# A column of weights turned by block transposes on VectorE, and a reordered head, in a three-layer cross network

## The chip, the cores and the metric

The kernel runs on one core of a Trainium2 chip. The time is the device time of one execution in microseconds (us); medians are given with the lowest and highest run. All times in this document are of one core, so the state of a whole die plays no part, and every profiled run was a fast one with a mean granted TensorE clock of 0.995 to 1.0. Each experiment ran beside the kernel before on the same chip. TensorE multiplies matrices, VectorE and GpSimd do elementwise work, ScalarE does copies, squares and biases, SyncE issues most transfers. SBUF is the on-chip memory, PSUM the accumulators that TensorE writes.

## The reference

```python
B, F, E = 2048, 64, 16            # this input has 1024 rows of x
h = x                             # (B, 64, 16), float32
for i in range(3):                # W[i] has 128 outputs
    z = einsum('bfe,bge->bfge', x, h).reshape(B, F * fh, E)
    y = einsum('oc,bce->boe', W[i], z) + b[i]
    x_i, h = (y[:, :64], y[:, 64:]) if i < 2 else (y, y)
    xs.append(x_i)
out = concatenate(xs, axis=1).sum(axis=2) @ fc_w.T + fc_b
```

Of the last layer only the sum with the fc weights is wanted. The kernel therefore folds these weights into W2 (called V2, 64 x 64), folds V2 into W1 (called M, kept in DRAM), and needs only products of x with shifted copies of itself, contracted with W0's half and with M.

## The kernel before

The rows are cut into 32 chunks of 32. The first 75 us, the *head*, handle four chunks (c0 to c3 below are `HEAD`, numbers 2, 3, 0, 1) while the weights are still being made. For each chunk and each of four shifts j, `product` makes a tile z of 128x2048 and `half_contract` multiplies it with W0's half on TensorE. A product's second input xb is either a shifted copy made by TensorE in PSUM (c0, c1) or loaded from DRAM into SBUF (c2, c3).

```python
keep_clock(8)                                   # zeros times zeros
...
h1_weights(0, w0o[0])                           # W0's weights of j = 0: one addition on VectorE
product(c0, 0, 2, NI)
nc.scalar.copy(w0o[1], w0s[1][:, :, 1, :])
h1_weights(1, w0o[1])
product(c0, 2)
...
for j in range(NJ - 1):
    product(c1, j)
product(c1, NJ - 1, engine=nc.gpsimd)

v2r = flat_tile("v2r")[:, 0:1024].rearrange("p (n c) -> p n c", n=2)
for n in range(2):
    pv = ps.tile([128, 512], F32, tag=("y", "set")[n], name=f"pv2_{n}")
    for k in range(4):                          # fc weights times W2: V2, as rows
        nc.tensor.matmul(pv[32 * k : 32 * k + 32], fv2, w2s[n][:, k * 512 : (k + 1) * 512], ...)
    nc.scalar.copy(v2r[:, n, :], pv)
half_contract(c1, 0)

pt = ps.tile([128, F // 4, 4], F32, tag="y", name="pt")
v2q = v2r.rearrange("p n (s o) -> p (n s) o", o=F)
for q in range(F // 4):                         # 32 matmuls with a 0/1 matrix turn rows to columns
    for to in halves:
        nc.tensor.matmul(pt[to, q, :], v2q[:, q, :], pick, start=True, stop=True)
nc.scalar.copy(v2t, pt.rearrange("p q k -> p (q k)"))
half_contract(c1, 3)

# M = V2 folded into W1: 8 matmuls, 4 copies to m_sb
for j in (1, 2):
    half_contract(c1, j)
# m_sb is written to DRAM (md) in pieces, and read back skewed (ms)
head_acc(c2)
for j in range(NJ):
    product(c2, j)
for j in range(NJ):
    half_contract(c2, j)
# ... reads of ms
for j in range(NJ):
    product(c3, j)
for j in range(NJ):
    half_contract(c3, j)
keep_h1()                                       # the squares of the diagonal
```

## Time and profile before

| | before |
|---|---|
| device time, median of 3 | 491.67 us (491.55 to 491.69) |
| span of the profiled run | 489.6 us |
| TensorE, VectorE, ScalarE, GpSimd busy | 484.7, 368.4, 90.5, 11.1 us |
| squares of the head start (the end of its contractions) | 44.59 us |
| first full contraction after the head | 59.09 us |

The span is what the profile sees from the first to the last instruction; the device time is some 1.8 us longer. The lines behind these numbers are shown in the prediction. They are read like this: the chain that ended last is followed back from the last instruction, and 99% of it lies on TensorE. So only what leaves TensorE's path, or lets it start sooner, can shorten the run, and that can be no more than the change takes out of the first 75 us.

### The profile page before, as it was taken

How to read it: one execution, taken by the hardware profiler on the slowest of the kernel's cores; microseconds unless marked ns; L12 is line 12 of the kernel's file. 1: busy time of each engine (PE TensorE's matmuls, PEld its weight loads, DVE VectorE, ACT ScalarE, POOL GpSimd, SP SyncE). 2: the span in 40 equal slices, each digit the busy share in tenths (PEclk: the TensorE clock that was granted, in tenths of full speed). 3: DMA queues.
4: the chain of work that ended last, by engine and by line, in shares of the span. 5: the costliest groups of instructions: out<-in, count | busy, mean ns of one | idle time of the engine just before them, and what ended most of it. 6: DMA issues, size and time to landing. Idle time of an engine off the chain costs nothing.

```text
span 489.6 us, 4089 instructions
## 1 busy us (share of the span) xinstructions
PE 484.7 (99%) x1696; PEld 219.4 (45%) x1696; DVE 368.4 (75%) x226; ACT 90.5 (18%) x157; POOL 11.1 (2%) x19
## 2 busy tenths in 40 slices
PE   9999999999999999999999999999999999999996
PEld 5655344343244344444444344443444434444474
DVE  5796899998899988898677686767868676780311
ACT  3224302022111122112211012212022121010001
POOL 5300000000000000000000000000000000000000
PEclk9999999999999999999999999999999999999999
DMA  8977984543846263544233344333244440000000
GB/s 338 420 244 220 382 347 171 173 171 112 321 182 242 93 252 143 199 171 173 106 116 138 156 171 171 149 138 106 122 173 171 171 167 5 0 0 0 1 0 1
DMA packets 14242, 78.59 MB, mean 161 GB/s; under 512 B 3756, under 2 KB 4428, under 8 KB 5200
## 3 DMA queue, kind: packets, MB, share of 16 engines
q1 hardware_dynamic: 13084, 77.05, 41.1%
q10 hardware_dynamic: 1140, 1.29, 0.9%
q8 instruction: 13, 0.21, 0.2%
q14 instruction: 5, 0.04, 0.0%
HBM read 76.69 MB, written 1.64 MB: 160 GB/s over the span
## 4 chain that ended last, share of the span: by engine, by line
PE 99%; DVE 0%; ACT 0%; issue 0%; POOL 0%; POOLq 0%
PE acc L250 79%; PE acc L284 6%; PE q L323 6%; PE acc L272 3%; PE acc L260 2%; PE misc L105 1%; PE xp L185 1%; PE po L623 0%; PE pm L451 0%; PE pv L427 0%; PE q L272 0%; PE pt L441 0%; PE q L334 0%; PE y L277 0%; PE acc L305 0%; DVE uu L355 0%
## 5 line engine op out<-in xcount | busy, mean ns | idle before, releaser
L250 PE MATMUL acc<-z,w_all 128*128 128x512 f32 (+1 forms) x928 | 387.6, 579 | 0.0
L216 DVE TENSOR_TENSOR z<-xa,xb 128x2048 f32<-128x2048 f32 x128 | 287.8, 2285 | 49.9 <-PE acc L250 40.4
L250 PEld LDWEIGHTS acc<-z,w_all 128*128 128x128 f32 x928 | 175.4, 190 | 210.9 <-issue 207.8
L221 ACT ACTIVATE z<-xa 32x512 f32<-32x512 f32 x34 | 21.3, 625 | 329.1 <-DVE z L216 327.3
L355 DVE SCALAR_TENSOR_TENSOR uu<-acc,vs,q 64x512 f32<-64x512 f32 (+1 forms) x29 | 21.2, 732 | 59.9 <-ACT q L354 59.7
L284 PE MATMUL acc<-z,w_all 128*64 128x256 f32 x256 | 28.7, 381 | 0.0
L323 PE MATMUL q<-z,w_all 128*64 128x512 f32 x128 | 27.9, 594 | 0.0
L354 ACT COPY q<-acc 64x512 f32<-64x512 f32 (+1 forms) x29 | 16.4, 565 | 36.5 <-PE acc L250 22.9
L284 PEld LDWEIGHTS acc<-z,w_all 128*64 128x64 f32 x256 | 17.9, 137 | 11.1 <-issue 2.5
L364 DVE TENSOR_REDUCE acc<-uu 128x64 f32<-128x1024 f32 (+3 forms) x19 | 20.3, 1072 | 0.3
L233 ACT COPY xx<-xa 64x512 f32<-64x512 f32 x32 | 19.6, 613 | 0.5
L229 ACT ACTIVATE sq<-xa 32x512 f32<-32x512 f32 x28 | 17.6, 628 | 0.6
L216 DVE TENSOR_TENSOR z<-xa,xp 128x2048 f32<-128x2048 f32 (+2 forms) x8 | 13.6, 1747 | 5.2 <-PE xp L185 5.2
L323 PEld LDWEIGHTS q<-z,w_all 128*64 128x64 f32 x128 | 9.0, 137 | 18.3 <-issue 18.0
L277 PE MATMUL y<-xx,bd 64*64 64x512 f32 x64 | 15.5, 603 | 0.0
L272 PE MATMUL acc<-xx,v1w 64*64 64x512 f32 (+1 forms) x58 | 13.5, 587 | 0.0
L360 DVE SCALAR_TENSOR_TENSOR uu<-y,cx,xx 128x512 f32<-128x512 f32 x16 | 11.4, 747 | 0.3
L216 POOL TENSOR_TENSOR z<-xa,xb_gps 128x2048 f32<-128x2048 f32 x2 | 9.1, 4555 | 4.8 <-ACT xb_gps L380 2.9
L260 PE MATMUL acc<-sq,w_sq 32*128 32x512 f32 (+1 forms) x58 | 8.0, 623 | 0.0
L272 PEld LDWEIGHTS acc<-xx,v1w 64*64 64x64 f32 x58 | 3.6, 132 | 8.9 <-issue 8.8
L105 PE MATMUL misc<-bd 128*128 128x128 f32 x28 | 5.0, 347 | 1.0 <-POOL bd L99 1.0
L105 PEld LDWEIGHTS misc<-bd 128*128 128x128 f32 x28 | 4.5, 251 | 1.8 <-POOL bd L99 1.0
(63 smaller groups left out, 65.2 us busy)
## 6 DMA issues: line engine op xcount, KB each, us to landing
xa<-in_xra SPq DMA_DIRECT2D x32, 1024.0 KB, 5.0
xb<-in_xrb SPq DMA_DIRECT2D x32, 1024.0 KB, 7.1
w<-in_w2t SPq DMA_DIRECT2D x2, 1024.0 KB, 9.9
xa<-in_xra SPq DMA_DIRECT2D x2, 768.0 KB, 6.2
w1s<-in_w1h SPq DMA_DIRECT2D x1, 1024.0 KB
w1x<-in_wx SPq DMA_DIRECT2D x1, 1024.0 KB, 9.4
w0x<-in_wx SPq DMA_DIRECT2D x1, 1024.0 KB, 7.0
w0t<-in_w0r SPq DMA_DIRECT2D x1, 768.0 KB, 6.3
```

Of the source, the lines that this page charges most:

```text
L216: engine.tensor_tensor(zs[c, j][:, at, :], xas[c][:, at, :], xbs[c][j].unsqueeze(1).to_broadcast([128, last - first, N]), ALU.mult,)
L221: nc.scalar.activation(zs[c, j][SQ, 0, :], xas[c][SQ, 0, :], AF.Square)
L229: nc.scalar.activation(sqs[c // 4][at : at + 32], xas[c][0:32, 0, :], AF.Square)
L233: nc.scalar.copy(xxs[c // 2][to], xas[c][to, 0, :])
L250: nc.tensor.matmul(acc_c, w_all[:, t, w_cols(c)], zs[c, j][:, i, cols], start=(t == 0 and c % 4 < 2), stop=(t == NT - NI and c % 4 >= 2),)
L260: nc.tensor.matmul(acc_c, w_sq[at, w_cols(c)], sqs[first // 4][at, cols], start=(r >= 2), stop=(r < 2), tile_position=(32 * r, 0),)
L272: nc.tensor.matmul(acc_c[q], v1w[rows], xxs[k][rows, cols], start=False, stop=(c >= FIRST and c % 4 < 2), skip_group_check=True,)
L284: nc.tensor.matmul(accs[c][halves[n]], w_all[:, t, 0:64], zs[c, j][:, i, n * H2 : (n + 1) * H2], start=(t == 0), stop=False,)
L323: nc.tensor.matmul(q_accs[k][halves[1 - n]], w_all[:, t, 64:128], zs[2 * k + n, j][:, i, :], start=(t == 0), stop=False,)
L354: nc.scalar.copy(q[h, cols], acc_c[64 - h.start : 128 - h.start])
L355: nc.vector.scalar_tensor_tensor(uu[:, cols], acc_c[h], bh1[h], q[h, cols], ALU.add, ALU.mult)
L364: nc.vector.tensor_reduce(acc[rows, of, k, half], uus[k][rows, of, E * half.start : E * half.stop].rearrange("p k (b e) -> p k b e", e=E), ...
```

## The change

Its intent: take the 32 pick matmuls off TensorE by transposing V2 in 32x32 blocks on VectorE; start M at once afterwards; and let VectorE, which then has less time, begin the third chunk sooner and hand one more product to GpSimd. The diff, cut to its core:

```diff
     def load_xb(c, first=NJ):
-        nc.sync.dma_start(out=xb, in_=xrb[c])
+        for at in (slice(0, first), slice(first, NJ)):
+            if at.start < NJ:
+                nc.sync.dma_start(out=xb[:, at, :], in_=xrb[c, :, at, :])
...
     nc.sync.dma_start(out=w0t[:, 0, :], in_=wh)
+    load_xa(c1, slice(0, 1))
     nc.sync.dma_start(out=w0t[:, 1:NJ, :], in_=w0r)
...
-    load_chunk(c2)
+    load_xa(c2)
+    load_xb(c2, 1)
...
-    keep_clock(8)
+    keep_clock(3)          # and the 2 matmuls of a constant (the biases' share of the output), moved here from 73 us
...
-    h1_weights(1, w0o[1])
     product(c0, 2)
+    h1_weights(1, w0o[1])
...
-    for j in range(NJ - 1):
+    for j in (0, 1):
         product(c1, j)
...
-        nc.scalar.copy(v2r[:, n, :], pv)
+        nc.vector.transpose(v2r[:, n, :], pv)
+    v2q = v2r.rearrange("p n (s r) -> p (n s) r", r=32)[:, :, 0]
+    for h in range(2):
+        at = slice(32 * h, 32 * h + 32)
+        nc.vector.tensor_copy(v2t[halves[h], at], v2q[halves[h]])
+        nc.scalar.copy(v2t[halves[1 - h], at], v2q[halves[h]])
+    product(c1, 2)
     half_contract(c1, 0)
-    pt = ...               # the pick matmuls, their copy, and half_contract(c1, 3)
     # M
-    for j in (1, 2):
+    for j in (3, 1, 2):
         half_contract(c1, j)
...
+    for j in (0, 1):       # two of the fourth chunk's xb go to PSUM
+        xb3 = ps.tile([128, N], F32, tag="y", name=f"xp_{c3}_{j}")
+        nc.scalar.copy(xb3, xbs[c3][j])
+        xbs[c3][j] = xb3
...
-    for j in range(NJ):
+    product(c3, NJ - 1, engine=nc.gpsimd)
+    for j in range(NJ - 1):
         product(c3, j)
-    for j in range(NJ):
+    for j in (0, 1, 3, 2):
         half_contract(c3, j)
```

W2's order in DRAM changes to suit, and M's four PSUM buffers are chosen anew.

More of the change, by code (lines that the diff above doesn't have):

```diff
@@ L115, in cin_kernel @@
         )
-    pick = const_tile("pick", [128, 4])
-    nc.gpsimd.memset(pick, 0.0)
-    for k in range(4):
-        nc.gpsimd.memset(pick[32 * k : 32 * k + 1, k : k + 1], 1.0)
     ones = const_tile("ones", [128, 2])
@@ L145, in load_xa, with load_xb @@
         )
-    def load_xb(c):
+    def load_xb(c, first=NJ):
         xb = xp.tile([128, NJ, N], F32, tag="xb", name=f"xb_{c}")
-        nc.sync.dma_start(out=xb, in_=xrb[c])
+        for at in (slice(0, first), slice(first, NJ)):
+            if at.start < NJ:
+                nc.sync.dma_start(out=xb[:, at, :], in_=xrb[c, :, at, :])
         xbs[c] = [xb[:, j, :] for j in range(NJ)]
@@ L162, in cin_kernel @@
     nc.sync.dma_start(out=w0t[:, 0, :], in_=wh)
+    load_xa(c1, slice(0, 1))
     nc.sync.dma_start(out=w0t[:, 1:NJ, :], in_=w0r)
+    load_xa(c1, slice(1, 4))
     w0s = [w0t[:, j, :].rearrange("p (i v g) -> p i v g", v=2, g=F) for j in range(NJ)]
     xb_gps = xp.tile([128, NJ, N], F32, tag="xb", name="xb_gps")
-    load_xa(c1, slice(0, 1))
-    load_xa(c1, slice(1, 4))
     for k in range(2):
@@ L193, in cin_kernel @@
     shift_pair(c0, (2, 3))
-    keep_clock(8)
+    keep_clock(3)
+    cst = const_tile("cst", [2, 1])
+    for j in range(2):
+        nc.tensor.matmul(
+            misc[0:2, 0:1], fcol[:, j : j + 1].to_broadcast([128, 2]), bcol[:, j : j + 1],
+            start=(j == 0), stop=(j == 1),
+        )
     acc = const_tile("acc", [128, 2, NCH // 2, CB])
@@ L390, in cin_kernel @@
     product(c0, 0, 2, NI)
+    nc.scalar.activation(cst, misc[0:2, 0:1], AF.Identity, bias=fcb, scale=float(E))
     nc.scalar.copy(w0o[1], w0s[1][:, :, 1, :])
+    product(c0, 2)
     h1_weights(1, w0o[1])
-    product(c0, 2)
     for j in (2, 3):
@@ L431, in cin_kernel @@
             )
-        nc.scalar.copy(v2r[:, n, :], pv)
-    half_contract(c1, 0)
-    pt = ps.tile([128, F // 4, 4], F32, tag="y", name="pt")
-    v2q = v2r.rearrange("p n (s o) -> p (n s) o", o=F)
-    for q in range(F // 4):
-        for to in halves:
-            nc.tensor.matmul(pt[to, q, :], v2q[:, q, :], pick, start=True, stop=True)
-    nc.scalar.copy(v2t, pt.rearrange("p q k -> p (q k)"))
-    half_contract(c1, 3)
+        nc.vector.transpose(v2r[:, n, :], pv)
[5 more added lines that the diff above has]
+    product(c1, 2)
+    half_contract(c1, 0)
     m_sb = z_tile("m_sb")
-    pms = [ps.tile([128, N], F32, tag=("set", "y")[m // 2], name=f"pm_{m}") for m in range(NI)]
+    pms = [
+        ps.tile([128, N], F32, tag=tag, name=f"pm_{m}", bufs=4 if tag == "acc" else 2)
+        for m, tag in enumerate(("acc", "set", "y", "y"))
+    ]
     for m in (0, 1):
@@ L601, in cin_kernel @@
     cx = const_tile("cx", [128, 1])
-    cst = const_tile("cst", [2, 1])
     def biases():
-        pb = ps.tile([128, 2], F32, tag="set", name="pb")
-        pcx, pc = pb[:, 0:1], pb[0:2, 1:2]
+        pcx = ps.tile([128, 1], F32, tag="set", name="pcx")
         for to in halves:
             nc.tensor.matmul(pcx[to], v2t[0:64], bh2, start=True, stop=True)
-        for j in range(2):
-            nc.tensor.matmul(
-                pc, fcol[:, j : j + 1].to_broadcast([128, 2]), bcol[:, j : j + 1],
-                start=(j == 0), stop=(j == 1),
-            )
         nc.scalar.copy(cx, pcx)
-        nc.scalar.activation(cst, pc, AF.Identity, bias=fcb, scale=float(E))
     NP = NCH // 2
@@ L755 @@
         "w1h": w1q,
-        "w2t": w2.reshape(128, 2, 8, 4, F).transpose(1, 0, 3, 2, 4).reshape(2, 128, 32 * F),
+        "w2t": w2.reshape(128, 2, 2, 16, 2, 32).transpose(2, 0, 1, 4, 3, 5).reshape(2, 128, 32 * F),
         "wx1": summed(w1[:64]),
```

## The prediction

No run had shown a transpose yet: the times given for the copies into v2t and in rival B rest on the author's estimate of its length. Lengths that the trace of before does show are 0.684 us for VectorE's 128x512 product with one input in PSUM, and for a 128x2048 product 2.285 us on VectorE and 4.555 on GpSimd. That the two engines can hold each other up (rival A) was an assumption then, which the trace of before does not show.

> **What bounds the kernel now.** I read the busy table first, then the chain that ended last, then the timeline of the first 75 us, because every line of the change lies there.
>
> ```profile
> PE 484.7 (99%) x1696; PEld 219.4 (45%) x1696; DVE 368.4 (75%) x226; ACT 90.5 (18%) x157; POOL 11.1 (2%) x19
> PE 99%; DVE 0%; ACT 0%; issue 0%; POOL 0%; POOLq 0%
> ```
>
> TensorE is busy from 1.0 us to the end, and the chain never leaves it for more than the last 2 us. But busy is not the same as useful: a wait of a few tenths hides between pipelined matmuls. So I take the chain in order of time (start, length, what), where each piece is a stage of the head:
>
> ```profile
> 3.93 2.11 PE xp L185 x16
> 6.04 1.98 PE misc L105 x16
> 8.02 1.88 PE acc L284 x16
> 9.90 2.75 PE xp L185 x16
> 12.64 5.33 PE acc L284 x48
> 17.97 1.85 PE pv L427 x16
> 19.83 1.88 PE acc L284 x16
> 21.70 1.81 PE pt L441 x63
> 23.52 1.78 PE acc L284 x16
> 25.30 1.88 PE pm L451 x16
> 27.18 17.42 PE acc L284 x160
> 44.59 0.62 PE acc L305 x16
> 73.23 0.17 PE pb L610 x4
> ```
>
> A half contraction (one j of a head chunk) costs 1.73 to 1.88 us, ten of them 17.42. Three pieces are not contraction: the 8 clock-keepers at 6.04 (zeros times zeros), the 32 pick matmuls at 21.70, the constant at 73.23. And the second shift, at 9.90, takes 2.75 where the first takes 2.11 [...]: it holds a wait. The timeline (start, length, engine, what, idle before and its releaser) names it, and shows VectorE at the places that matter:
>
> ```profile
> 7.24 1.21 DVE L216 TENSOR_TENSOR z<-xa,xp 128x1024 f32<-128x1024 f32 x1
> 9.23 2.28 DVE L216 TENSOR_TENSOR z<-xa,xp 128x2048 f32<-128x2048 f32 x1
> 11.56 0.20 PEld L185 LDWEIGHTS xp<-xa,shift 64*64 64x64 f32 x4 [0.69 <-DVE z L216]
> 24.71 6.70 DVE L216 TENSOR_TENSOR z<-xa,xb 128x2048 f32<-128x2048 f32 x3 [3.50 <-DMA xb<-in_xrb]
> ```
>
> The last shift waits for a PSUM buffer until product 2 of the first chunk ends (9.23 + 2.28 = 11.51). VectorE then stands idle 3.5 us until the third chunk's xb lands at 24.7. From there it works nearly without a break to 42.3 (8 products at a pitch of 2.20 us), so the products of chunks three and four leave little room if TensorE comes sooner.
>
> [...] 12 records of clock-keepers take 2.93 us at the start, 16 take 1.98 at 6 us. [...] both GpSimd products (5.99 to 10.54, 12.47 to 17.03) lie beside products whose xb is in PSUM.
>
> **The change part by part.**
>
> *Clock-keepers, 8 to 3, plus the constant's 2 matmuls.* A matmul leaves two records, a keeper's 0.111 us apart in the trace, so three end at about 6.65, the constant at about 6.85. The first contraction then waits for its weights (VectorE 6.91 + 0.42 = 7.33) and starts at 7.40 instead of 7.95. Its tiles i = 0, 1 take 0.86; i = 2 needs the product that ends at 7.24 + 1.21 = 8.45, so it resumes at 8.52 and the shift starts near 9.48 instead of 9.83. Gain here 0.35, but the next wait swallows it.
>
> *Product 2 before the second weight sum.* VectorE goes straight from 8.42 into product 2, done at 10.70 instead of 11.51; the sum follows to 11.1. The shift's first pair ends at 10.4; its last matmul waits for the later of the two buffers, 11.15 instead of 11.57. Net gain at the start of the next contraction: 0.42, in place of the 0.35, not on top. W0's rest lands some 0.6 us later (256 KB at 420 GB/s), about 9.0, still before its sum at 10.7. VectorE is 0.4 us ahead from here.
>
> *V2.* 32 pick matmuls go: their piece runs from 21.54 to 23.37 = 1.84 us of TensorE. In their place: two transposes instead of two ScalarE copies of 0.59, then four small copies of about 0.2 in two pairs. pv is ready at about 18.6 and 19.45 (17.9 - 0.42, plus the 1.13 and 1.99 after which ScalarE could read it before). VectorE has finished two products of the second chunk by 18.6. [...] copies to 20.6. The contraction that runs meanwhile ends near 21.2, so v2t is 0.6 us early and the whole 1.84 is won.
>
> *M before j = 3.* The order only; M starts at 21.2 instead of 25.2, m_sb is complete at 24.3 instead of 28.4. TensorE's sum is unchanged. The two weight writes on SyncE's queue still stand behind the fourth chunk's xb, so M's weights gain perhaps 1.5 us, not 4. They need no more: the first sum of them was done at 42.75, needed at 45.14 before and at about 42.85 now.
>
> *VectorE's order afterwards.* Product 2 of chunk two: 20.6 to 22.85. xb's first quarter lands about 22.7 (xa's end near 22.1 plus 0.6), so the third chunk starts at 22.9 instead of 24.7: products at 25.1, 27.3, 29.5, 31.8. TensorE reaches them at 28.2, 30.0, 31.7, 33.4. In the fourth chunk j = 0, 1 take their xb from PSUM, done at 34.0 and 36.2, wanted at 35.2 and 36.9; GpSimd's j = 3 runs beside them from 31.8 to 36.4, wanted at 38.6; j = 2 to 38.6, wanted at 40.4. Every product is in time, the least slack 0.7 us. Without the GpSimd product the fourth on VectorE would end at 40.8 plus its square, too late for 40.4.
>
> *The constant at 73 us:* 0.17 less, pure gain.
>
> Sum: 0.42 + 1.84 + 0.17 = 2.4 us, all on TensorE's path; nothing after 75 us is touched. 491.67 - 2.4 = 489.2.
>
> **The rivals.** *A, GpSimd and VectorE lock each other.* If the fourth chunk's xb lands before product 3 of the third chunk starts (29.5), [...] that product then waits for 4.55 us and TensorE stalls 3 to 4 us: 492 to 493. For it: nothing in the program holds GpSimd back, only the transfer. Against: xb landed about 29.7 before, with M's writes now sharing the DMA engines it lands later, and VectorE's products follow one another with no gap. I give it one in six. *B, M waits.* If the transposes took twice my estimate, v2t would come at 21.9 and 0.7 us be lost; likewise if pm's buffer is one that product 2 of chunk two holds until 22.85 (0.8 lost). 490.0. *C, fed too late.* If M's writes push the fourth xb beyond 32, its PSUM copies (0.6 each) and products are late by as much, less the slack: 489.5 to 490.5. *D, the head holds more than I see:* if the shift's last wait vanishes entirely, 0.3 more: 488.9. A change of 2% (9.8 us) would need a stall or a gain as long as a fifth of the head; none is in sight.
>
> **Range and chances.** 489.2 if all goes as worked out; B and C make 490, A up to 493. The lower end has only timings of tenths: 488.5. I set the range at 488.5 to 491.2, somewhat skewed upwards. Chances: faster by over 2% 0.01, within 2% 0.98, slower 0.01.
>
> **What would show it.** The pick group is gone and pm starts near 21.2; the piece that was 2.75 is about 2.65 and ends near 12.2; the ten contractions from j = 3 on take 5.2 and 12.2 without a wait; the squares' matmuls (0.62) start near 42.2 instead of 44.59; [...] GpSimd's third product lasts 4.55 us and starts when the third chunk's last product ends. I am wrong if a weight load of the contractions waits for a product over half a microsecond, if GpSimd's product lasts much over 4.6, or if a VectorE product lasts much over 2.3.

## The result, and the profile after

| | before | after |
|---|---|---|
| device time, median | 491.62 us (491.55 to 491.94), 6 runs | 489.1 us (489.07 to 489.2), 6 runs |
| span | 489.6 us | 487.3 us |
| TensorE busy | 484.7 us | 482.3 us |
| squares of the head start | 44.59 us | 42.39 us |
| first full contraction | 59.09 us | 56.90 us |

The ratio is 0.9948, with a 95% interval of 0.9935 to 0.9961: the same within 2%, half a per cent faster. Here and below a ratio is the mean time of one kernel's fast runs over that of the other's in the same rounds, so it is not quite the ratio of the medians quoted.

The changed kernel's busy table and the shares of its chain, by engine:

```profile
PE 482.3 (99%) x1622; PEld 216.4 (44%) x1622; DVE 367.6 (75%) x229; ACT 90.7 (19%) x158; POOL 16.6 (3%) x15
PE 99%; DVE 0%; ACT 0%; issue 0%; POOL 0%; POOLq 0%
```

TensorE is still the bound, with 2.4 us less of work: the number that the prediction's sum gives. Its chain in order of time (start, length, what; the line numbers shift by a few, so L284 of before is L291 here, L427 is L436, L451 is L462):

```profile
3.93 3.33 PE xp L184 x16
7.26 0.86 PE misc L105 x6
...
8.30 1.88 PE acc L291 x16
10.17 2.14 PE xp L184 x16
12.31 5.33 PE acc L291 x48
17.64 1.85 PE pv L436 x16
19.50 1.88 PE acc L291 x16
21.37 1.88 PE pm L462 x16
23.25 19.14 PE acc L291 x176
42.39 0.62 PE acc L312 x16
...
70.83 0.21 PE pcx L622 x4
```

The pick group is gone and M (pm) follows the first contraction of the second chunk directly, at 21.37. Then comes one unbroken piece of 11 half contractions, 19.14 us or 1.74 each; ten took 17.42 before. So no contraction waits for a product. The three steps can be read off against the chain in the prediction: the contraction of j = 1 starts at 12.31 instead of 12.64, which is 0.33; the squares start 2.20 earlier, so V2's part is 1.87; the constant that stood behind the last but one line is gone, 0.17. Together 2.4.

The timeline of the changed kernel (start, length, engine, what, idle time before it and its releaser) shows who feeds that piece:

```profile
18.70 1.58 DVE L441 STREAM_TRANSPOSE v2r<-pv 128x512 f32<-128x512 f32 x2
20.75 2.29 DVE L223 TENSOR_TENSOR z<-xa,xp 128x2048 f32<-128x2048 f32 x1
22.95 8.89 DVE L223 TENSOR_TENSOR z<-xa,xb 128x2048 f32<-128x2048 f32 x4
30.39 5.89 POOL L223 TENSOR_TENSOR z<-xa,xb 128x2048 f32<-128x2048 f32 x1 [13.06 <-DMA xb<-in_xrb]
31.76 4.48 DVE L223 TENSOR_TENSOR z<-xa,xp 128x2048 f32<-128x2048 f32 x2
36.16 2.28 DVE L223 TENSOR_TENSOR z<-xa,xb 128x2048 f32<-128x2048 f32 x1
```

The third chunk's products start at 22.95, not 24.71, and follow one another to 31.85. Then come two products with xb in PSUM, and one more. One line is odd. GpSimd's product lasts 5.89 us, while its other two last 4.56. It starts at 30.39, in the middle of VectorE's last product of the third chunk (29.56 to 31.85), and ends at 36.28. That is 4.43 after VectorE's product ended. So the record holds 1.3 to 1.5 us (5.89 less 4.56, or 31.85 less 30.39) in which GpSimd did not get on with its product, as in the prediction's rival A, and it was VectorE's product that went first. From here on "the lock" is the name for what the records of these runs show: of two products, one on each engine and both with two SBUF inputs, one did its work only when the other had ended, and its record is longer by the wait (here 5.89 us instead of 4.56). The products with xb in PSUM do not take part: the first of them runs beside GpSimd's in 2.28. Most of the experiments go after what happens when the order is the other one.

### The profile page after: what moved, and what is told of

The parts are those of the page before. It is cut to its first block, busy times and chain, and to the rows that moved or that the text cites. A ratio compares the mean times of both kernels' runs of the same rounds, so it can differ in the third digit from the quotient of the medians.

```text
span 487.3 us, 3939 instructions
## 1 busy us (share of the span) xinstructions
PE 482.3 (99%) x1622; PEld 216.4 (44%) x1622; DVE 367.6 (75%) x229; ACT 90.7 (19%) x158; POOL 16.6 (3%) x15
## 4 chain that ended last, share of the span: by engine, by line
PE 99%; DVE 0%; ACT 0%; issue 0%; POOL 0%; POOLq 0%
PE acc L257 79%; PE acc L291 6%; PE q L330 6%; PE acc L279 3%; PE acc L267 2%; PE xp L184 1%; PE misc L105 1%; PE po L631 0%; PE pm L462 0%; PE pv L436 0%; PE q L279 0%; PE q L341 0%; PE y L284 0%; PE acc L312 0%; DVE uu L362 0%
## 5 line engine op out<-in xcount | busy, mean ns | idle before, releaser
L223 DVE TENSOR_TENSOR z<-xa,xb 128x2048 f32<-128x2048 f32 x125 | 281.0, 2285 | 45.9 <-PE acc L257 38.6
L362 DVE SCALAR_TENSOR_TENSOR uu<-acc,vs,q 64x512 f32<-64x512 f32 (+1 forms) x29 | 21.2, 731 | 59.9 <-ACT q L361 59.7
L291 PE MATMUL acc<-z,w_all 128*64 128x256 f32 x256 | 28.5, 381 | 0.0
L361 ACT COPY q<-acc 64x512 f32<-64x512 f32 (+1 forms) x29 | 16.4, 565 | 36.5 <-PE acc L257 22.9
L291 PEld LDWEIGHTS acc<-z,w_all 128*64 128x64 f32 x256 | 18.0, 137 | 11.2 <-issue 2.5
L223 DVE TENSOR_TENSOR z<-xa,xp 128x2048 f32<-128x2048 f32 (+2 forms) x10 | 18.1, 1856 | 5.9 <-PE xp L184 5.9
L284 PE MATMUL y<-xx,bd 64*64 64x512 f32 x64 | 15.5, 603 | 0.0
L223 POOL TENSOR_TENSOR z<-xa,xb 128x2048 f32<-128x2048 f32 x1 | 5.9, 5890 | 13.1 <-DMA xb<-in_xrb 13.1
L184 PE MATMUL xp<-xa,shift 64*64 64x512 f32 x32 | 5.6, 803 | 0.0
```

Of the source, the lines that this page charges most:

```text
L223: engine.tensor_tensor(zs[c, j][:, at, :], xas[c][:, at, :], xbs[c][j].unsqueeze(1).to_broadcast([128, last - first, N]), ALU.mult,)
L291: nc.tensor.matmul(accs[c][halves[n]], w_all[:, t, 0:64], zs[c, j][:, i, n * H2 : (n + 1) * H2], start=(t == 0), stop=False,)
L361: nc.scalar.copy(q[h, cols], acc_c[64 - h.start : 128 - h.start])
L362: nc.vector.scalar_tensor_tensor(uu[:, cols], acc_c[h], bh1[h], q[h, cols], ALU.add, ALU.mult)
```

## The experiments

Theory: the gain is 1.84 us from V2, 0.4 from the head's order and 0.17 from the constant, and the early xb, the new order and GpSimd's third product are there so that V2's part is not lost again. Rivals: V2 gains all by itself; or the gain comes from elsewhere; and, for the danger, GpSimd's product could block VectorE if it comes first. All twelve kernels gave correct results. They ran in three groups of four, each on a chip of its own beside the kernel before: v2_alone, v2_undone, xb_whole and xb_in_sbuf (before: 491.62 us); after_again, v2_undone_j3, whole_held and sum_first (before: 491.67); and the rest (before: 491.71).

### v2_alone: V2's part put into the kernel before

```diff
 # against before
-        nc.scalar.copy(v2r[:, n, :], pv)
+        nc.vector.transpose(v2r[:, n, :], pv)
-    pt = ...                                  # the pick matmuls and their copy
+    # the four small copies into v2t, as in the change; W2's order in DRAM too
```

> The kernel before with the V2 part alone: block transposes and four copies in place of the 32 pick matmuls, everything else as before. Theory: TensorE's own work falls by 1.84 us, but the rest of the change is what keeps it fed. In the kernel before the last product of the fourth chunk ends at 42.42 us and TensorE reaches it at 42.7; nothing here moves that product, so TensorE arrives at 40.9 and waits some 1.5 us in the fourth chunk: 491.2 to 491.5, hardly faster than before. Rival: the removed matmuls are the gain and the rest is ornament: 489.8.

Measured: 491.37 us (490.99 to 493.09, 14 runs), ratio 0.9997 (0.9989 to 1.0005). The interval holds 1, so no gain is shown, though the pick matmuls are gone. (The profiled run, 490.99, is the fastest of the 14.) The timeline of this kernel, TensorE alone, with the idle time in brackets:

```profile
39.88 1.95 PE L279 MATMUL acc<-z,w_all 128*64 128x256 f32 x16 [0.25 <-DVE z L211]
42.08 1.95 PE L279 MATMUL acc<-z,w_all 128*64 128x256 f32 x16 [0.25 <-DVE z L211]
```

Its chain, at the squares:

```profile
44.03 0.62 PE acc L300 x16
```

At the end of the fourth chunk TensorE now waits for products: its last two contractions start 2.20 us after the one before (37.68, 39.88, 42.08), which is VectorE's pitch, not their own 1.74. M starts at 23.68 instead of 25.30: the 1.84 of V2, less 0.25 by which this run's head was late (the contraction of j = 1 starts at 12.89, not 12.64). But the squares start at 44.03 instead of 44.59. Of the 1.62 us in hand at M, 0.56 are left; 1.06 went into waits for products, which did not exist before. In the medians V2 alone is worth 0.25 us, which the interval doesn't tell from nothing; with the rest of the change the chain keeps all of the 1.84.

### v2_undone and v2_undone_j3: the whole change, with the pick matmuls put back

```diff
 # against after
-        nc.vector.transpose(v2r[:, n, :], pv)
+        nc.scalar.copy(v2r[:, n, :], pv)
-    # the four small copies into v2t
     product(c1, 2)
     half_contract(c1, 0)
+    pt = ...                                  # the pick matmuls and their copy
+    half_contract(c1, 3)                      # v2_undone_j3 only; it then runs (1, 2) after M
```

> The changed kernel with V2 turned by the 32 pick matmuls again, the rest of the change kept. Theory: the whole of the 1.84 us comes back on TensorE, nothing else waits: 490.9, and the contractions show no wait. Rival: the gain came from feeding TensorE better and not from its work, so 489.5 or less.

Measured: 492.33 us (491.96 to 493.97, 21 runs, three of them above 493.7), ratio 1.0019 (1.0013 to 1.0026). The mean granted clock of those three was 0.996; they have no trace. The median is 3.2 more than the changed kernel's, not 1.84. Its chain:

```profile
21.47 1.84 PE pt L457 x63
...
23.33 0.22 ACT v2t L458
...
44.68 0.62 PE acc L317 x16
```

The picks cost the 1.84, and as M follows them at once it also waits for ScalarE's copy of v2t (0.22 and its neighbours). The squares start 2.29 us later than in the changed kernel. The second form hides that copy behind a contraction:

> The changed kernel with V2 turned by matmuls again, and with j = 3 of the second chunk between the pick matmuls and M, as in the kernel before. The variant without that order came out at 492.3; its trace shows 1.84 us of pick matmuls, 0.3 us of wait for v2t behind them, and an output transfer 0.8 us longer than in the other runs. Theory: the 1.84 us alone remain, 490.9. Rival: undoing V2 costs more than its matmuls (3 us) wherever M stands, 492.

Measured: 492.0 us (491.58 to 492.72, 13 runs), ratio 1.0006 (0.9998 to 1.0014). In its chain the picks take 1.81 and the squares start at 44.55, 2.16 later than in the changed kernel: 1.81 from the picks and some 0.3 from the head, where the contraction of j = 1 starts at 12.60 instead of 12.31. The span is 2.9 longer, so 0.75 comes at the very end, and 0.8 in v2_undone. There the last output write lands 1.90 us after its issue (1.81 in v2_undone_j3) instead of 1.08. In both traces an 8 KB packet of the instruction queue starts just before the last output packets; in the changed kernel it comes after them. That the two belong together is argued from the order alone; no run isolates it. So the 1.84 is confirmed in the chain, and the other 1.1 us of the second form are a head that varies and a tail that the theory did not have.

### after_again: the changed kernel once more

Its profile was also to show whether the longer first shift (16 records in 3.33 us in the changed kernel, 2.11 before) belongs to the kernel or to the run.

> The changed kernel unaltered, as the yardstick of these rounds: 489.1. [...] the shift may take 2.1 here and the contraction of j = 1 starts near 12.15 instead of 12.31, with the time the same to 0.2 us.

Measured: 489.06 us, ratio 0.9952 (0.994 to 0.9964). Thirteen of 14 runs lie between 488.86 and 489.20, and one at 493.09. The profiled run has the same order as before: GpSimd's record from 30.80, VectorE's last product of the third chunk from 29.54, 1.26 us ahead. The records of the first shift's matmuls have a median of 914 ns here and of 1057 in the first profile of the same kernel, so its length is not fixed by the kernel; the contraction of j = 1 starts at 12.29. The one slow run has no trace. A loss of its size, 4 us, is what the next experiments make on purpose.

### xb_whole: the third chunk's xb in one transfer

```diff
-    load_xb(c2, 1)
+    load_xb(c2)
```

Two cases are on record for GpSimd's product, which was to be ready before the last of VectorE's products in SBUF: in the first it waits until that series has ended, in the second it starts between two products of the series.

> The changed kernel with the third chunk's xb loaded in one transfer. VectorE starts that chunk at 24.65 instead of 22.96, 1.7 us late; its least slack after is 0.86 us (product 1 of the fourth chunk, 36.24 against 37.1), so TensorE waits 0.85 us: 489.9 to 490.0. GpSimd's product is ready near 30.3, now with one more two-SBUF product of VectorE to come after the running one. [...] GpSimd's record is stretched to end near 38.1 and nothing more is lost. [...] product 3 of the third chunk is held for 4.5 us and the time is 493 to 494. Rival: the split is ornament: 489.1.

Measured: 494.91 us (494.64 to 496.0, 5 runs), ratio 1.007 (1.0057 to 1.0083), slower than the kernel before. The third chunk starts 1.5 us later, at 24.48, so the fourth chunk's xb lands well before the third chunk's last product starts. From the timeline:

```profile
29.74 5.82 POOL L223 TENSOR_TENSOR z<-xa,xb 128x2048 f32<-128x2048 f32 x1 [11.78 <-DMA md<-m_sb]
37.76 10.54 PE L291 MATMUL acc<-z,w_all 128*64 128x256 f32 x80 [3.31 <-DVE z L223]
```

And from the chain:

```profile
31.09 6.62 DVE z L223
```

GpSimd's product waits through VectorE's third product and then goes ahead *between* two back-to-back VectorE instructions: VectorE's fourth product has a record from 31.09 to 37.72, 6.62 us instead of 2.28. It ends 2.15 us after GpSimd's (29.74 + 5.82 = 35.56), so it did its work only then. TensorE stands for 3.31 us. That VectorE had no gap was no protection here.

The wait has a second price. The windows view (stretch, its length, TensorE busy, granted clock, DMA share and GB/s):

```profile
34.40:37.80 3.40, 0.09 (x4) 1.00 0.14 39
37.80:41.20 3.40, 3.40 (x16) 0.50 0.66 161
```

After the wait the granted clock is 0.50 for 3.4 us, and the first contraction takes 3.46 us (37.76 to 41.22) where the next takes 1.73. In three other profiles the first contraction after such a wait was not slow: it took 1.95 us in the timeline, as one without a wait does (before, at 19.76), after 2.48 us in keep_8, 2.49 in enablers_old and 3.04 in xb_in_sbuf, and the mean granted clock of each of these runs was 1.0 (0.995 in xb_whole). The squares are 5.9 us later than in the changed kernel (48.30 against 42.39): 0.7 is a head that was late in this run, 1.7 the halved clock, and 3.5 the wait with its restart.

### xb_in_sbuf: no copies of the fourth chunk's xb into PSUM

```diff
-    for j in (0, 1):
-        xb3 = ps.tile([128, N], F32, tag="y", name=f"xp_{c3}_{j}")
-        nc.scalar.copy(xb3, xbs[c3][j])
-        xbs[c3][j] = xb3
```

The first case on record is that GpSimd's product waits until the whole series of VectorE's products has ended.

> The changed kernel without the two copies of xb into PSUM, so that VectorE's products of the fourth chunk all read two SBUF inputs while GpSimd's product waits or runs. [...] they end at 38.5 as now, GpSimd's product ends only near 43, TensorE waits about 4 us for it: 493.2. If GpSimd gets in at the end of the third chunk's last product: it ends at 36.4 as now, a product of VectorE starts or ends 4.5 us late (38.7): 492.8. If there is no lock worth the name: 489.1, with both engines at their usual durations.

Measured: 493.94 us (492.75 to 494.57, 5 runs), ratio 1.0043 (1.0031 to 1.0055). Here GpSimd (record from 30.30, 6.48 long) gets in when the third chunk is done, and the fourth chunk's first product, now with both inputs in SBUF, takes from 32.32 to 38.93, 6.61 us. TensorE waits 3.04 us for it. In the changed kernel the product in the same place has its xb in PSUM and ran beside GpSimd's in 2.28. So the copies are what lets the two engines work at once.

### whole_held: xb_whole, but GpSimd made to wait

```diff
 # against xb_whole
+    held = const_tile("held", [1, 1])
+    nc.gpsimd.tensor_copy(held, zs[c2, NJ - 1][0:1, 1, 0:1])
     product(c3, NJ - 1, engine=nc.gpsimd)
```

The added copy of one element reads the result of the third chunk's last product, so GpSimd cannot start before it.

> The variant with xb in one transfer (494.9), with one tiny GpSimd copy before GpSimd's product that makes it wait for product 3 of the third chunk. If the 5 us lost there are the lock, in which GpSimd slips in between two products of VectorE, then this wait gives all but the late start back: no product of VectorE over 2.3 us, GpSimd's product 4.6 us from about 33.5, and 489.9 to 490.1 in all. If the loss was the late xb itself, the time stays near 494.9.

Measured: 490.16 us (490.07 to 490.33, 5 runs), ratio 0.9969 (0.9957 to 0.998). From the timeline:

```profile
33.77 0.17 POOL L540 COPY held<-z 1x1 f32<-1x1 f32 x1 [16.53 <-DVE z L223]
33.94 4.55 POOL L223 TENSOR_TENSOR z<-xa,xb 128x2048 f32<-128x2048 f32 x1
38.02 2.62 DVE L223 TENSOR_TENSOR z<-xa,xb 128x2048 f32<-128x2048 f32 x1
```

Adding a wait gained 4.7 us; part of that is the halved clock and the late head, which this run does not have. GpSimd's product has its own length again, and the late third chunk costs only 1.1 against the changed kernel. The last VectorE product, with both inputs in SBUF, meets GpSimd's end and is held for 0.34 (2.62 instead of 2.28). This is the test that separates the lock from a late transfer: the third chunk starts even later than in xb_whole (24.80 against 24.48), and the fourth chunk's xb again lands a microsecond before the third chunk's last product (30.37 against 31.42), so that without the wait GpSimd would have come first. What differs is the order of the two products.

### sum_first: the second weight sum before product 2, as before

```diff
-    product(c0, 2)
-    h1_weights(1, w0o[1])
+    h1_weights(1, w0o[1])
+    product(c0, 2)
```

> The changed kernel with the second weight sum before product 2 again, as in the kernel before, the load order kept. W0's rest lands near 9.15 us, so VectorE now stands idle from 8.65 to 9.6; product 2 ends near 12.2 instead of 10.85, the shift's last matmul waits for it, and the contraction of j = 1 starts 1.0 us late: 490.1. If only the order mattered as in the kernel before (0.4): 489.5. If nothing there is on the path: 489.1.

Measured: 493.97 us (493.83 to 494.5, 5 runs), ratio 1.0049 (1.0036 to 1.0062). The contraction of j = 1 starts at 13.58, 1.3 late: W0's rest lands later now that a slice of x goes ahead of it, the sum waits for it, and product 2 behind the sum. So the early slice and the new order belong together. The other 3.6 us are the lock again. VectorE is late by about 1.3 throughout, GpSimd's record starts at 29.68, the last product of the third chunk only at 30.83, and that one lasts 6.62.

### no_gpsimd: the fourth chunk all on VectorE

```diff
-    product(c3, NJ - 1, engine=nc.gpsimd)
-    for j in range(NJ - 1):
+    for j in range(NJ):
         product(c3, j)
-    for j in (0, 1, 3, 2):
+    for j in range(NJ):
         half_contract(c3, j)
```

> The changed kernel with all four products of the fourth chunk on VectorE, in the order 0, 1, 2, 3, and the contractions in that order. From the profile after, VectorE would end them at 34.05, 36.24, 38.45 and 40.65, and TensorE wants them at 35.4, 37.1, 38.8 and 40.6, with the square needed only for the tile taken last: 489.1 to 489.3 in the median, and no run near 493, because there is no lock to fall into. If the product on GpSimd is needed as the prediction says (the fourth product and its square too late): 489.5 or more.

Measured: 489.46 us (489.31 to 489.66, 5 runs), ratio 0.9951 (0.9939 to 0.9963). The weight loads of the last contraction, from the timeline:

```profile
41.02 1.49 PEld L291 LDWEIGHTS acc<-z,w_all 128*64 128x64 f32 x16 [0.49 <-DVE z L223]
```

The wait shown is that of the weight loads. The 11 contractions take 19.40 us in the chain (23.57 to 42.97) instead of 19.14, so about a quarter of a microsecond is what the third GpSimd product buys. The median is 0.4 higher than the changed kernel's in the other rounds; in the profiled run 0.3 of the difference is a later head (the contraction of j = 1 starts at 12.63). The gain is small beside what it puts at risk.

### enablers_old and keep_8: two small parts undone

```diff
 # enablers_old: the slice of x after W0's rest again, j = 3 before M again
-    load_xa(c1, slice(0, 1))
     nc.sync.dma_start(out=w0t[:, 1:NJ, :], in_=w0r)
+    load_xa(c1, slice(0, 1))
+    half_contract(c1, 3)
     # M
-    for j in (3, 1, 2):
+    for j in (1, 2):
 # keep_8
-    keep_clock(3)
+    keep_clock(8)
```

> The changed kernel with two of its orders put back: the second chunk's first x slice after W0's rest, and j = 3 of the second chunk before M. Neither is on TensorE's path by the profile after (x slice wanted at 10.1, landed at 9.1 in the kernel before; the first M weights ready at 38.9, wanted at 43.0), so 489.1. But M's writes then leave later and delay the fourth chunk's xb less: it may land near 29.7 instead of 30.2, only 0.1 to 0.2 us after product 3 of the third chunk starts (29.54). A good part of the runs, or all, may then lose the 4 us of the lock: 493.

Measured: median 489.31 us over 22 runs, ratio 0.9987 (0.9967 to 1.0006). But no run lies near the mean: 12 are at 489.04 to 489.39 and 10 at 492.71 to 494.25. The profiled run is one of the slow kind:

```profile
29.62 4.55 POOL L223 TENSOR_TENSOR z<-xa,xb 128x2048 f32<-128x2048 f32 x1 [12.14 <-DMA xb<-in_xrb]
25.29 11.03 DVE L223 TENSOR_TENSOR z<-xa,xb 128x2048 f32<-128x2048 f32 x3
36.38 1.95 PE L291 MATMUL acc<-z,w_all 128*64 128x256 f32 x16 [2.49 <-DVE z L223]
```

GpSimd won by 0.07 us: its product starts at 29.62 or 29.63, VectorE's last of the third chunk at 29.70, and lasts 6.63 (three products in 11.03 us; they take 6.69 in the changed kernel). GpSimd, first this time, has its plain 4.55.

> The changed kernel with 8 clock-keepers again. The contraction of j = 1 cannot start before 12.29, where VectorE's product 2 lets it. [...] 8 keepers end near 8.1 and nothing is lost: 489.1. With the slow first shift they end near 9.4, the contraction starts near 13.2: 490.0. In no case are the 5 keepers worth the 1.1 us that they take.

Measured: median 493.88 us over 22 runs, ratio 1.0011 (0.999 to 1.0032), again in two groups: 8 at 488.99 to 489.63 and 14 at 493.1 to 494.49. The good runs lose nothing by the five keepers, as theory had it. In the profiled run, a slow one, the contraction of j = 1 is 0.28 late (12.59), VectorE's products with it, and GpSimd wins by 0.14 (29.70 against 29.84). The chain doesn't lead to the keepers, though: it comes from the landing of W0's first quarter, which ScalarE takes up at 6.97 instead of 6.69. And the fourth chunk's xb was there sooner, at 29.50 instead of 30.19. Nothing in this trace ties either to the keepers, so that they cause the slow runs is not shown.

### later_sum_held: a candidate

```diff
-    keep_clock(3)
+    keep_clock(6)
-    h1_weights(0, w0o[0])
     product(c0, 0, 2, NI)
+    h1_weights(0, w0o[0])
+    held = const_tile("held", [1, 1])           # as in whole_held
+    nc.gpsimd.tensor_copy(held, zs[c2, NJ - 1][0:1, 1, 0:1])
```

> A candidate to beat the changed kernel: GpSimd's product of the fourth chunk held by a tiny copy until product 3 of the third chunk is done, and the first weight sum after the first chunk's whole product 0 instead of before its second half, so that VectorE does not wait for W0's head; 6 keepers fill TensorE's longer wait. Product 2 should end 0.4 to 0.5 us sooner, the contraction of j = 1 start near 12.0 instead of 12.3: 488.8, and no run near 493.

Measured: 489.03 us (488.85 to 489.3, 5 runs), ratio 0.9944 (0.9931 to 0.9956). The contraction of j = 1 starts at 12.15 and the squares at 42.23, each 0.16 sooner than in the changed kernel, and GpSimd's product lasts 4.57. It ties with the changed kernel in the median; the two intervals overlap. What it adds is that GpSimd's product can no longer precede the third chunk's last. Five runs without a slow one would not show that, since at a rate of one in 20 there would be none in five with a chance of 0.95^5 = 77%; the dependency does.

### The race in one table

The profiled run of each kernel, and its own time. The third column is where VectorE's last product of the third chunk starts.

| kernel | GpSimd's record starts | VectorE's product starts | that product lasts | time |
|---|---|---|---|---|
| after | 30.39 | 29.56 | 2.28 | 489.07 |
| after_again | 30.80 | 29.54 | 2.28 | 489.06 |
| enablers_old | 29.62 | 29.70 | 6.63 | 492.86 |
| keep_8 | 29.70 | 29.84 | 6.63 | 493.1 |
| sum_first | 29.68 | 30.83 | 6.62 | 493.97 |
| xb_whole | 29.74 | 31.09 | 6.62 | 494.91 |

The product that got in first kept its own length (VectorE's 2.28 in the first two kernels, GpSimd's 4.55 in enablers_old and 4.61 in keep_8), and the other's record took in the wait (GpSimd's 5.89 and 5.46, VectorE's 6.63). In sum_first and xb_whole GpSimd's record starts while an earlier product of VectorE runs; it lasts 5.62 and 5.82 and ends 4.47 after VectorE's next product starts, so it waited for the running one alone. The changed kernel's margin was 0.83 us in one profile and 1.26 in the other, before a loss of about 4 us.

GpSimd's record starts 0.2 us after the fourth chunk's xb lands, which is when ScalarE begins to copy it (30.39 and 30.19 in the changed kernel, 29.62 and 29.43 in enablers_old). In no_gpsimd, whose loads are those of the changed kernel:

```profile
29.63 1.11 ACT L499 COPY xp<-xb 128x512 f32<-128x512 f32 x2 [2.10 <-DMA xb<-in_xrb]
```

VectorE's last product of the third chunk starts there at 29.88. A GpSimd product, 0.2 us after the landing, would have come at about 29.83 (an estimate from the other traces): the race would have been lost or tied with the changed kernel's own loads. In later_sum_held, on the same chip, the same copies start at 31.25. So the landing varies by more than the margin, and the changed kernel itself was not run in the rounds of enablers_old and keep_8. That the chip of these rounds, and not the edits, makes the slow runs so frequent (10 and 14 of 22) is a rival that no run excludes.

Within each slow group the slower runs have a mean granted clock of 0.995 to 0.997 (in enablers_old those from 493.45 up), the others 0.998 to 1.0 (up to 493.16). That fits the halved clock seen in xb_whole, which then follows some of the waits and not all; those runs have no trace.

## Why the prediction was right

The predicted 489.2 against 489.1 is a hit, and it holds by its parts.

- **Clock-keepers and product 2.** The step said 0.42; 0.33 was measured (12.64 to 12.31), in one pair of profiles. The same head started this contraction at 12.29 to 13.00 in the other profiles that keep it, as W0's first quarter was there at 6.6 to 7.4, so a match to a tenth is in part luck. On the way its working was off. The first contraction started at 8.30, not 7.40, because the first shift took longer: 3.33 us instead of 2.11, the median of its matmuls' records 1057 ns instead of 590, with the granted clock at 1.00 in both. Over the runs it took from 1.88 to 3.51, so it is a property of the run. The next wait, for the buffer of product 2, swallowed that, as the step said it would swallow the keepers' 0.35. The whole of VectorE was some 0.2 later than worked out because W0's first quarter was there at 6.69 instead of 6.50, which by itself would account for the missing 0.09.
- **V2.** The step said 1.84; the chain gives 1.87, and 1.81 to 1.84 when the matmuls are put back. The transposes took 0.718 us each, somewhat more than the author's estimate and than the 0.684 of the 128x512 product, and v2t was still in time: M started at 21.37, predicted near 21.2.
- **M's weights.** The step said 1.5 us earlier; the first sum came 3.8 earlier (38.50 instead of 42.34). M landed in DRAM 1.8 earlier; the first sum itself stood behind VectorE's last product in both kernels (42.42 and 38.44), and that product ends sooner because GpSimd has one. This term was mis-sized, but it was not on the path.
- **VectorE's order afterwards.** The products came within 0.2 of the times given (third chunk at 22.95, predicted 22.9; GpSimd's end at 36.28, predicted 36.4). "Without the GpSimd product the fourth on VectorE would end at 40.8 plus its square, too late" was right in kind: no_gpsimd loses about a quarter of a microsecond there.
- **The constant.** 0.17, gone from the chain.
- **Two signs that failed.** The ten contractions that the text counts after M, in 5.2 and 12.2 us, are eleven (3 and 8); they took 19.14 us together, and the start of the squares had been worked out with all eleven. And the text named a GpSimd product of much over 4.6 us as a sign of being wrong. It lasted 5.89 and the time was right: the record counts the wait for VectorE's product, so the sign should have been VectorE's product over 2.3 us.
- **Rival A.** What it described was right: four experiments show it in profiles, with a VectorE product of 6.62 or 6.63 us, and it fits the one run in 20 at 493.09. Its size, 492 to 493, was somewhat low: such runs of enablers_old and keep_8 took 492.7 to 494.5, and the granted clock of 0.50 after the wait (xb_whole) was not in the sum. But an argument against it was wrong: "VectorE's products follow one another with no gap" does not keep GpSimd out, as xb_whole shows. What kept it out was the landing of xb after 29.56. The other argument, that M's writes delay the landing, is not shown: with j = 3 before M and so the writes later, GpSimd started at 29.62 in enablers_old instead of 30.39, but in no_gpsimd and keep_8, with M first, xb was there at 29.63 and 29.50 as well. That the landing came late enough in the changed kernel is luck, not something that the program ensures.
- **Rivals B, C and D** did not occur: v2t was in time, xb landed at 30.17 rather than beyond 32, and the second shift still held a wait (2.14 us against 1.88 without).

Open remain the trace of a slow run of the unchanged kernel after, its true rate (one of 20, none of them in the rounds of the two bimodal kernels), what makes xb land sooner or later, and the cause of the output's extra 0.8 us in the two kernels with the picks restored.

## What to carry to other kernels

Work removed from the engine that bounds a kernel pays only if its feeders can keep the new pace: V2 alone gained 0.25 us of its 1.84 in the medians, not told from nothing, and with the reordering of loads and products the rest came too. Where GpSimd and VectorE both read two SBUF operands, as in the products here that took turns (2.28 us became 6.62), fix their order with a real dependency rather than by when a transfer happens to land; in the kernel with the late third chunk one tiny added wait turned a loss of 3.3 us against before into a gain of 1.5. And look at all runs, not the median alone: two kernels here with medians of 489.31 and 493.88 are the same two groups of times in different shares.
